# Splitting fp32 operands into words: a ScalarE rounding in place of a VectorE bit mask

## The chip, the cores and the metric

The kernel runs on one core of a Trainium2 chip. A core has five engines that run side by side[...]: TensorE (matmuls; PE in the profile), VectorE (DVE), ScalarE (ACT), GpSimd (POOL) and SyncE, which here only issues DMA. The metric is the time of one execution on the device, in microseconds (us). Before the change it is 3097.36 us, the median of 2 runs (3093.87 to 3100.86). The profile is of one execution with a span of 3092.7 us.

## The reference

A graph layer on 64 graphs of 256 nodes with 768 features, all in fp32. Cut to what matters:

```python
h = maximum(layernorm(x), 0)
ctx = adj @ (h @ Wadj.T + badj) / deg          # adj: 64 x 256 x 256 integers
ctx += adj.T @ (h @ Wrev.T + brev) / rdeg
ctx += h @ Wself.T + bself
out = x + ctx + (terms of the relations)
```

The three 768x768 weights make most of the work. The kernel computes the three weight products as one block product with fewer multiplications than blocks (a scheme of 15 products of sums of blocks). For each graph the left operands are sums of 128-row blocks `a0, a1, a2, b0, b1, b2`, and the right operands are sums of weight blocks, 256 columns wide. The products are made in two sweeps over the 64 graphs: the first makes the aggregates and 8 of the products, and keeps the operands and partial sums in DRAM; the second reloads them and makes the other 7.

## The kernel before

In the second sweep four of the seven products of a graph (9, 7, 15 and 4) are not made as fp32 matmuls but out of shorter words in the type `fp32r`. `split_left` cuts a left operand `value` (128 partitions x 768 fp32) in three words, and it is what the change touches:

```python
def split_left(b, n):
    value = S[b]["L"][PRODUCTS[n][0]]
    words = []                       # three word tiles, from a rotation of three sets of buffers
    for tag in LEFT_WORDS[len(left_words) % 3]:
        ...
    top = pool2.tile([P, F, P], F32, tag="top", name=f"top{n}_{b}")                # SBUF, 2 buffers
    nc.vector.tensor_scalar(top.bitcast(I32), value.bitcast(I32), FIRST, None, op0=ALU.bitwise_and)
    nc.scalar.activation(words[0], top, AF.Copy)
    nc.vector.tensor_tensor(words[1], value, top, op=ALU.subtract)
    nc.vector.scalar_tensor_tensor(words[2], words[1].bitcast(F32), -STEP, top, op0=ALU.mult, op1=ALU.add)
```

`split_right` does the like for the four weight operands, once each, in steps 0 and 1 of the second sweep. The products use the words thus:

```python
def product_first(b, n, ps):                   # 12 short-word matmuls into a PSUM bank
    for k in range(2):
        for f in range(F): nc.tensor.matmul(ps, l[k][:, f, :], r[2 * k][:, f, :], ...)
    nc.scalar.activation(ps, ps, AF.Copy, scale=1.0 + 1.0 / STEP)

def product(b, n, ps, start, row=None):        # 6 more onto the same bank, or 6 in fp32
    ...
def add_out(b, ps, sign, c, n, many=1):        # VectorE: o in SBUF +- a PSUM bank
    nc.vector.tensor_add(o, o, ps)             # or tensor_sub
```

One step of the second sweep (M is the graph being multiplied, A = M+1 the one being prepared; k counts the rows of `ORDER2`, where a product with `None` as its last entry is its `product_first`):

```python
ORDER2 = ((7, "v", None, None), (9, "x", None, ...), (15, "u", None, None), (7, "v", ...), (6, "x", ...),
          (15, "u", ...), (4, "t", None, None), (12, "x", 4, ...), (4, "t", ...), (9, "x", None, None), (1, "x", 5, ...))
for k, (n, *how) in enumerate(ORDER2):
    b = A if (n, how[-1]) == (9, None) else M
    if k == (2 if M < 2 else 0): combine_left(M, "a0+a2+b0+b2")       # GpSimd: one 128x768 addition
    if k == (3 if M == 0 else 0) and A < B: ahead2(A)                 # GpSimd: four more
    multiply(b, n, *how, 2)                                           # matmuls, then their add_out
    if M < 2 and n in WORDS and how[-1] is not None: split_right(n, M)
    if k == 1 and M > 1: split_left(M, 4)
    if 1 < A < B and k in (3, 5, 8): split_left(A, {3: 9, 5: 7, 8: 15}[k])
    ...
```

Products 6, 12 and 1 are plain fp32. Products 9, 6, 12 and 1 share the PSUM bank `x`: each of them adds onto what the last one left, so it must wait until VectorE has read the bank. Instructions go out in program order, and each engine takes its own in that order. The kernel's PSUM tiles are of one bank (2 KB per partition) each: three `q`, three of `ps1` (`pt`, `x`, `y`) and two of `ps2`, whose tile `pa` serves only the first sweep.

Of the kernel before, what the change touches and what calls it, by code (L numbers as in the profile page):

```python
# [9 lines left out]
F32 = mybir.dt.float32  # L10
F32R = mybir.dt.float32r
BF16 = mybir.dt.bfloat16
I32 = mybir.dt.int32
AF = mybir.ActivationFunctionType
ALU = mybir.AluOpType
AX = mybir.AxisListType

P = 128
EPS = 1e-5
NMEAN, RSTD, RDEG, RRDEG = 8, 9, 10, 11  # L20

FIRST = -4096
STEP = 4096.0

# [70 lines left out]
def kernel(  # L97
# [40 lines left out]
    nc = tc.nc  # L138
    B, L, H = x.shape
# [3 lines left out]
    F = H // P  # L143
    HO = H // 2
    NB = H // 3
# [17 lines left out]
    def main_path(main: ExitStack):  # L163
        pool1 = main.enter_context(tc.tile_pool(name="pool1", bufs=1))
        pool2 = main.enter_context(tc.tile_pool(name="pool2", bufs=2))
# [1 line left out]
        dram = main.enter_context(tc.tile_pool(name="dram", bufs=3, space=bass.MemoryType.DRAM))  # L167
        kept = main.enter_context(tc.tile_pool(name="kept", bufs=1, space=bass.MemoryType.DRAM))
        ps3 = main.enter_context(tc.tile_pool(name="ps3", bufs=3, space=bass.MemoryType.PSUM))
        ps2 = main.enter_context(tc.tile_pool(name="ps2", bufs=2, space=bass.MemoryType.PSUM))  # L170
        ps1 = main.enter_context(tc.tile_pool(name="ps1", bufs=1, space=bass.MemoryType.PSUM))

        W = {n: pool1.tile([P, F, NB], F32, name=f"w{n}") for n in PRODUCTS}
        rows = pool1.tile([P, len(ROWS), NB], F32R, name="rows")

        hilo = pool1.tile([P, 2, C, H], F32R, tag="hilo", name="hilo")
# [4 lines left out]
        def load_weights(products):  # L181
            for n in products:
                right = PRODUCTS[n][1]
                k, o = int(right[1]), int(right[2])
                v = (wadj_t, wrev_t, wself_t)[k].rearrange("(f p) o -> p f o", p=P)
                nc.sync.dma_start(W[n], v[:, :, ts(o, NB)])
# [49 lines left out]
        def prepare_rows():  # L236


            eT, brow, pick = (R[n] for n in ("eT", "brow", "pick"))
            wr = R["wr0"], R["wr1"]  # L240
            for k, at in ((0, 1), (1, NBASE + 1)):
                to = pick[:, k, :].rearrange("p (q r) -> p q r", q=4)[:, :, 3 + k]
                nc.scalar.activation(to, eT[:, at : at + 1].to_broadcast([P, 4]), AF.Copy)
            for n in range(2):
                pr = ps2.tile([P, 512], F32, tag="pa", name=f"pr{n}")
                for k in range(2):
                    nc.tensor.matmul(pr[:, :HO], pick[:, k, :], wr[k][:, ts(n, HO)], start=(k == 0), stop=(k == 1))
                nc.vector.tensor_add(brow[:, ts(n, HO)], brow[:, ts(n, HO)], pr[:, :HO])
# [37 lines left out]
        def load_sums(b, sweep):  # L286

            s = S[b]
            s["o"] = pool2.tile([P, C, H], F32, tag="o", name=f"o{sweep}_{b}")
            nc.sync.dma_start(s["o"], x_v[b] if sweep == 1 else s["sums"])  # L290
# [100 lines left out]

        def aggregate(b, f):
            s = S[b]
            pa = ps2.tile([P, 512], F32, tag="pa", name=f"pa_{b}_{f}")
            k = 0
            for c in range(C):
                for part in range(2):
                    nc.tensor.matmul(  # L398
                        pa, hilo[:, part, c, ts(f, P)], s["a"][:, c, :, :].rearrange("p s i -> p (s i)"),
                        start=(k == 0), stop=(k == 2 * C - 1),  # L400
                    )
                    k += 1
            nc.vector.tensor_mul(  # L403
                s["X"][:, f, :, :].rearrange("p s i -> p (s i)"), pa, s["row"][:, 2:4, :].rearrange("p s i -> p (s i)")
            )

        def combine_left(b, name, eng=None):

            L = S[b]["L"]
            x, op, y, home = {**LEFT1, **LEFT2}[name]  # L410
            if home in L:
                L[name] = L[home]
            else:
                L[name] = pool1.tile([P, F, P], F32, tag=home, name=f"{name}_{b}")
            (eng or nc.gpsimd).tensor_tensor(L[name], L[x], L[y], op=op)  # L415

        left_words, right_words = {}, {}

        def split_left(b, n):

            value = S[b]["L"][PRODUCTS[n][0]]
            words = []
            for tag in LEFT_WORDS[len(left_words) % 3]:
                many = 2 if tag == "x" else 1
                pool = pool2 if tag == "a" else pool1
                t = pool.tile([P, many, F, P], F32R, tag=tag, name=f"words{len(words)}_{n}_{b}")
                words += [t[:, k] for k in range(many)]
            top = pool2.tile([P, F, P], F32, tag="top", name=f"top{n}_{b}")
            nc.vector.tensor_scalar(top.bitcast(I32), value.bitcast(I32), FIRST, None, op0=ALU.bitwise_and)  # L429
            nc.scalar.activation(words[0], top, AF.Copy)  # L430
            nc.vector.tensor_tensor(words[1], value, top, op=ALU.subtract)  # L431
            nc.vector.scalar_tensor_tensor(words[2], words[1].bitcast(F32), -STEP, top, op0=ALU.mult, op1=ALU.add)  # L432
            left_words[b, n] = words

        def split_right(n, k):


            work = pool1.tile([P, 2, F, NB], F32, tag="hilo", name=f"work{n}_{k}")
            top, rest = work[:, 0], work[:, 1]
            names = [(f"w{m}", f"w{n}_{i}") for i, m in enumerate((*WORDS[n], n))]  # L440
            tiles = [pool1.tile([P, F, NB], F32R, tag=t, name=m) for t, m in (names[:2] if k == 0 else names[2:])]
            right_words.setdefault(n, []).extend(tiles)
            if k == 0:
                nc.vector.tensor_scalar(top.bitcast(I32), W[n].bitcast(I32), FIRST, None, op0=ALU.bitwise_and)
                nc.scalar.activation(tiles[0], top, AF.Copy)
            nc.vector.tensor_tensor(rest, W[n], top if k == 0 else right_words[n][0].bitcast(F32), op=ALU.subtract)
            if k == 0:
                nc.vector.scalar_tensor_tensor(tiles[1], top, -1.0 / STEP, rest, op0=ALU.mult, op1=ALU.add)
            else:
                nc.scalar.activation(tiles[0], rest, AF.Copy, scale=STEP)  # L450

        def product_first(b, n, ps):
            l, r = left_words[b, n], right_words[n]
            for k in range(2):
                for f in range(F):
                    nc.tensor.matmul(  # L456
                        ps, l[k][:, f, :], r[2 * k][:, f, :], start=(k == 0 and f == 0), stop=(k == 1 and f == F - 1)
                    )
            nc.scalar.activation(ps, ps, AF.Copy, scale=1.0 + 1.0 / STEP)

# [46 lines left out]
        def start():  # L507
# [19 lines left out]
            for f in range(F):  # L527
                aggregate(0, f)
# [87 lines left out]
        def front2(b):  # L616
            s = S[b]
            new_left(b, 2)
            nc.scalar.dma_start(s["X"], s["kept_X"])
            nc.scalar.dma_start(s["Xs"], s["kept_Xs"][:, :, 0, :])  # L620
            line = pool2.tile([P, P], F32, tag="line", name=f"line2_{b}")
            nc.sync.dma_start(line, s["line"])
            s["line2"] = line

        def step2(t):

            M, A = t, t + 1
            s = S[M]
            if A < B:
                load_sums(A, 2)  # L630
            if M > 1 and M + 2 < B:
                front2(M + 2)
            if M == 0:
                front2(1)
            s["tokT"] = pool3.tile([P, P], F32R, tag="tokT", name=f"tokT2_{M}")
            nc.scalar.activation(s["tokT"], s["line2"], AF.Copy)
            for k, (n, *how) in enumerate(ORDER2):
                b = A if (n, how[-1]) == (9, None) else M
                if k == (2 if M < 2 else 0):
                    combine_left(M, "a0+a2+b0+b2")  # L640
                if k == (3 if M == 0 else 0) and A < B:
                    ahead2(A)
                if b < B:
                    multiply(b, n, *how, 2)
                if M < 2 and n in WORDS and how[-1] is not None:
                    split_right(n, M)
                if k == 1 and M > 1:
                    split_left(M, 4)
                if 1 < A < B and k in (3, 5, 8):
                    split_left(A, {3: 9, 5: 7, 8: 15}[k])  # L650
                if how[-1] and n == 4:
                    store_sums(M, 0, 2)
            store_sums(M, 1, 2)
            if M < 2 and M + 2 < B:
                front2(M + 2)

        def ahead2(b):
            for name in ("a0+a2", "a1+a2", "a0+a2+b2", "b1+b2"):
                combine_left(b, name)
# [6 lines left out]
        for t in range(B):  # L666
            step1(t)
            if t == 0:
                load_weights((6, 4, 1))
        ahead2(0)  # L670
        for t in range(B):
            step2(t)
# [123 lines left out]
    with ExitStack() as main:  # L796
        with tc.manual_schedule():
            main_path(main)
# [36 lines left out]
```

## Time and profile before

| | first sweep (0 to 1800 us) | second sweep (2000 to 3000 us) |
|---|---|---|
| TensorE busy | 1725.44 us, 96% | 913.03 us, 91% |
| VectorE busy | 1023.40 us, 57% | 968.32 us, 97% |
| ScalarE busy | 522.13 us, 29% | 254.43 us, 25% |
| GpSimd busy | 1217.00 us, 68% | 605.41 us, 61% |
| DMA rate | 242 GB/s | 210 GB/s |

The busy time of an engine counts an instruction from its start to its end, so time in which a started instruction is held up counts as busy. In the lines of the profile, `L431 DVE TENSOR_TENSOR words<-X,top` is line 431 of the kernel, on VectorE, which writes `words` from `X` and `top`. L429 is the bit mask, L430 the ScalarE copy to the first word, L431 the subtraction, L432 the third word; L415 are the block sums on GpSimd, L456 the matmuls of `product_first`, L468 and L473 those of `product`, L459 the scaling on ScalarE, L481 and L483 the additions into `o`. The fp32 matmul of the program is two matmul instructions in the trace, so six of them show as "x12".

### The profile page before, as it was taken

Reading aid. Unit: us, or ns where it says so; the run is one execution under the profiler, and the core shown is the slowest. Engines: PE = TensorE matmul, PEld = TensorE weight load, DVE = VectorE, ACT = ScalarE, POOL = GpSimd, SP = SyncE. Lnnn points to the kernel's source line nnn. Section 1 sums busy time; section 2 is a strip of 40 time slices with the busy share of each in tenths; the row PEclk is TensorE's granted clock in tenths of the full one; section 3 lists DMA queues with packets and bytes.
Section 4 is the critical chain, followed back from the end, with each engine's and each line's share of the span. In section 5 each row is a group of like instructions: output and inputs, shape, how many; then the busy total and the mean of one; then the engine's idle time right before and its main releaser. Section 6 shows DMA issues by size and latency. Waiting matters only on the chain.

```text
span 3092.7 us, 39494 instructions
## 1 busy us (share of the span) xinstructions
PE 2882.7 (93%) x15002; PEld 2533.7 (82%) x15002; DVE 2220.7 (72%) x3220; ACT 836.7 (27%) x1797; POOL 1965.7 (64%) x905
## 2 busy tenths in 40 slices
PE   5799999999999999999999987999999999999998
PEld 3688888888888888888888876888888888888888
DVE  5655556555555555556565648999999999999997
ACT  3232233223233322323222302222222222222222
POOL 4567767666766777676666654566566565656563
PEclk8899999999999999999999998999999999999999
DMA  8677776777677677766666644655555565555553
GB/s 271 219 249 245 253 246 243 243 240 249 241 254 245 244 247 239 251 237 240 234 233 238 228 158 182 213 207 209 208 208 209 206 213 204 212 208 208 206 209 141
DMA packets 226442, 695.07 MB, mean 225 GB/s; under 512 B 17332, under 2 KB 94900, under 8 KB 209864
## 3 DMA queue, kind: packets, MB, share of 16 engines
q1 hardware_dynamic: 189384, 390.49, 38.1%
q10 hardware_dynamic: 36864, 302.01, 25.8%
q8 instruction: 120, 1.97, 0.3%
q14 instruction: 74, 0.61, 0.1%
HBM read 436.31 MB, written 256.11 MB: 224 GB/s over the span
## 4 chain that ended last, share of the span: by engine, by line
PE 50%; DVE 31%; issue 6%; POOL 5%; DMA 5%; ACT 3%; ACTq 0%; DVEq 0%; SPq 0%; POOLq 0%
PE y L468 17%; DVE words L431 10%; PE w L468 9%; PE pa L398 8%; PE z L468 7%; DVE words L432 6%; DVE top L429 5%; PE x L468 5%; POOL xT L389 5%; DVE o L481 4%; DMA row<-d 3%; PE v L456 1%; DVE o L483 1%; ACT a L307 1%; ACT Xs L390 1%
## 5 line engine op out<-in xcount | busy, mean ns | idle before, releaser
L415 POOL TENSOR_TENSOR X<-X,Xs 128x768 f32<-128x768 f32 x256 | 596.3, 2345 | 511.4 <-DVE words L431 426.9
L389 POOL TENSOR_TENSOR xT<-xT,row 128x1536 f32<-128x1536 f32 (+1 forms) x128 | 445.8, 3483 | 187.2 <-DMA row<-d 182.2
L468 PE MATMUL y<-w,X 128*128 128x256 f32 x2304 | 534.4, 382 | 2.8 <-POOL X L415 2.4
L468 PE MATMUL x<-w,X 128*128 128x256 f32 x1560 | 401.3, 411 | 126.6 <-DVE o L483 86.6
L468 PEld LDWEIGHTS y<-w,X 128*128 128x128 f32 x2304 | 431.2, 191 | 68.6 <-issue 3.5
L398 PE MATMUL pa<-a,hilo 128*128 128x512 f32 x1536 | 455.9, 433 | 26.3 <-DVE X L403 23.3
L468 PEld LDWEIGHTS x<-w,X 128*128 128x128 f32 x1560 | 309.5, 205 | 185.9 <-DVE o L483 98.8
L430 ACT ACTIVATE words<-top 128x768 fp32r<-128x768 f32 x248 | 209.6, 845 | 781.7 <-DVE top L429 781.7
L398 PEld LDWEIGHTS pa<-a,hilo 128*128 128x128 f32 x1536 | 294.4, 192 | 90.6 <-DVE X L403 25.0
L432 DVE SCALAR_TENSOR_TENSOR words<-words,top 128x768 fp32r<-128x768 f32 x248 | 349.4, 1409 | 8.6
L431 DVE TENSOR_TENSOR words<-X,top 128x768 fp32r<-128x768 f32 x186 | 343.7, 1848 | 6.4
L403 DVE TENSOR_TENSOR X<-pa,row 128x512 f32<-128x512 f32 x384 | 264.5, 690 | 115.6 <-PE pa L398 115.3
L390 ACT ACTIVATE Xs<-xT 128x1536 f32<-128x1536 f32 x64 | 95.1, 1485 | 845.5 <-POOL xT L389 845.5
L360 DVE SCALAR_TENSOR_TENSOR hilo<-x,cols,hilo 128x768 fp32r<-128x768 f32 x128 | 261.9, 2047 | 9.8 <-ACT hilo L363 9.7
L320 POOL TENSOR_TENSOR cols<-cols,half 128x2 f32<-128x2 f32 x64 | 44.8, 701 | 251.3 <-DVE cols L319 234.0
L429 DVE TENSOR_SCALAR top<-X 128x768 int32<-128x768 int32 x186 | 187.7, 1009 | 9.0 <-POOL X L415 9.0
L468 PE MATMUL y<-w,b0+b 128*128 128x256 f32 x768 | 178.0, 382 | 2.6 <-POOL b0+b L415 2.6
L468 PE MATMUL x<-w,Xs 128*128 128x256 f32 x768 | 177.0, 380 | 2.7 <-issue 2.7
L468 PE MATMUL z<-w,b2-a 128*128 128x256 f32 x768 | 176.2, 379 | 1.4 <-DVE w L212 1.4
L468 PE MATMUL z<-w,Xs 128*128 128x256 f32 x768 | 176.8, 380 | 0.0
L468 PE MATMUL w<-w,X 128*128 128x256 f32 x768 | 176.3, 379 | 0.0
L468 PE MATMUL w<-w,a1+b 128*128 128x256 f32 x768 | 176.2, 379 | 0.0
(120 smaller groups left out, 4834.1 us busy)
## 6 DMA issues: line engine op xcount, KB each, us to landing
kept_X<-X ACTq DMA_DIRECT2D x64, 1536.0 KB, 5.1
X<-kept_X ACTq DMA_DIRECT2D x64, 1536.0 KB, 7.0
x<-in_x_dram SPq DMA_DIRECT2D x64, 768.0 KB, 6.1
xT<-in_x_t_dram SPq DMA_DIRECT2D x64, 768.0 KB
o<-in_x_dram SPq DMA_DIRECT2D x64, 768.0 KB
kept_Xs<-Xs ACTq DMA_DIRECT2D x64, 768.0 KB, 6.6
sums<-o SPq DMA_DIRECT2D x128, 384.0 KB, 6.8
Xs<-kept_Xs ACTq DMA_DIRECT2D x64, 768.0 KB
```

The source lines that it names most:

```text
L360: nc.vector.scalar_tensor_tensor(lo, hx, rstd, hi.bitcast(F32), op0=ALU.mult, op1=ALU.subtract)
L389: eng.tensor_tensor(v, v, row[:, k : k + 1, :].to_broadcast([P, f1 - f0, L]), op=op)
L390: nc.scalar.activation(s["Xs"], xT, AF.Relu)
L398: nc.tensor.matmul(pa, hilo[:, part, c, ts(f, P)], s["a"][:, c, :, :].rearrange("p s i -> p (s i)"), start=(k == 0), stop=(k == 2 * C - 1),)
L403: nc.vector.tensor_mul(s["X"][:, f, :, :].rearrange("p s i -> p (s i)"), pa, s["row"][:, 2:4, :].rearrange("p s i -> p (s i)"))
L415: (eng or nc.gpsimd).tensor_tensor(L[name], L[x], L[y], op=op)
L429: nc.vector.tensor_scalar(top.bitcast(I32), value.bitcast(I32), FIRST, None, op0=ALU.bitwise_and)
L430: nc.scalar.activation(words[0], top, AF.Copy)
L431: nc.vector.tensor_tensor(words[1], value, top, op=ALU.subtract)
L432: nc.vector.scalar_tensor_tensor(words[2], words[1].bitcast(F32), -STEP, top, op0=ALU.mult, op1=ALU.add)
L468: nc.tensor.matmul(ps, l[:, f, :], r[:, f, :], start=(start and f == 0), stop=(row is None and f == F - 1), skip_group_check=not start,)
L481: nc.vector.tensor_add(o, o, ps)
```

## The change

The first word is no longer made by masking off low bits on VectorE and copying the masked value on ScalarE. ScalarE makes it from the operand itself: it multiplies with 1 - 2^-13 and rounds to `fp32r` as it writes. A second ScalarE instruction copies this word into a PSUM tile, `top`, and VectorE takes its second operand from there in both of its instructions. The aim is to take work off VectorE, and to leave each of its two instructions one operand in SBUF and one in PSUM. The two banks of `pa` are given back at the end of the first sweep, and `top` (3 KB per partition, one buffer in place of two) takes their place. `split_right` gets its first word the same way, but subtracts it from SBUF and makes no copy. The split of product 9 comes one place later in the order. The diff, cut to its core:

```diff
-FIRST = -4096
+LOWER = 1.0 - 2.0**-13
...
-        ps2 = main.enter_context(tc.tile_pool(name="ps2", bufs=2, space=bass.MemoryType.PSUM))
+        sweep = ExitStack()
+        ps_sums = sweep.enter_context(tc.tile_pool(name="ps_sums", bufs=2, space=bass.MemoryType.PSUM))
...                                                                # split_left
-            top = pool2.tile([P, F, P], F32, tag="top", name=f"top{n}_{b}")
-            nc.vector.tensor_scalar(top.bitcast(I32), value.bitcast(I32), FIRST, None, op0=ALU.bitwise_and)
-            nc.scalar.activation(words[0], top, AF.Copy)
+            top = ps_top.tile([P, F, P], F32, tag="top", name=f"top{n}_{b}")
+            nc.scalar.activation(words[0], value, AF.Copy, scale=LOWER)
+            nc.scalar.activation(top, words[0].bitcast(F32), AF.Copy)
             nc.vector.tensor_tensor(words[1], value, top, op=ALU.subtract)
             nc.vector.scalar_tensor_tensor(words[2], words[1].bitcast(F32), -STEP, top, op0=ALU.mult, op1=ALU.add)
...                                                                # split_right
-                nc.vector.tensor_scalar(top.bitcast(I32), W[n].bitcast(I32), FIRST, None, op0=ALU.bitwise_and)
-                nc.scalar.activation(tiles[0], top, AF.Copy)
-            nc.vector.tensor_tensor(rest, W[n], top if k == 0 else right_words[n][0].bitcast(F32), op=ALU.subtract)
+                nc.scalar.activation(tiles[0], W[n], AF.Copy, scale=LOWER)
+            first = right_words[n][0].bitcast(F32)
+            nc.vector.tensor_tensor(rest, W[n], first, op=ALU.subtract)
...                                                                # step2
-                if 1 < A < B and k in (3, 5, 8):
-                    split_left(A, {3: 9, 5: 7, 8: 15}[k])
+                if 1 < A < B and k in (4, 5, 8):
+                    split_left(A, {4: 9, 5: 7, 8: 15}[k])
...                                                                # between the sweeps
+        sweep.close()
+        ps_top = main.enter_context(tc.tile_pool(name="ps_top", bufs=1, space=bass.MemoryType.PSUM))
```

More of the change, by code (lines that the diff above doesn't have):

```diff
@@ L244, in prepare_rows @@
             for n in range(2):
-                pr = ps2.tile([P, 512], F32, tag="pa", name=f"pr{n}")
+                pr = ps_sums.tile([P, 512], F32, tag="pa", name=f"pr{n}")
                 for k in range(2):
@@ L393, in aggregate @@
             s = S[b]
-            pa = ps2.tile([P, 512], F32, tag="pa", name=f"pa_{b}_{f}")
+            pa = ps_sums.tile([P, 512], F32, tag="pa", name=f"pa_{b}_{f}")
             k = 0
@@ L435, in split_right @@
         def split_right(n, k):
-            work = pool1.tile([P, 2, F, NB], F32, tag="hilo", name=f"work{n}_{k}")
-            top, rest = work[:, 0], work[:, 1]
+            rest = pool1.tile([P, F, NB], F32, tag="hilo", name=f"work{n}_{k}")
             names = [(f"w{m}", f"w{n}_{i}") for i, m in enumerate((*WORDS[n], n))]
@@ L443, in split_right @@
             if k == 0:
-                nc.vector.tensor_scalar(top.bitcast(I32), W[n].bitcast(I32), FIRST, None, op0=ALU.bitwise_and)
-                nc.scalar.activation(tiles[0], top, AF.Copy)
-            nc.vector.tensor_tensor(rest, W[n], top if k == 0 else right_words[n][0].bitcast(F32), op=ALU.subtract)
+                nc.scalar.activation(tiles[0], W[n], AF.Copy, scale=LOWER)
+            first = right_words[n][0].bitcast(F32)
+            nc.vector.tensor_tensor(rest, W[n], first, op=ALU.subtract)
             if k == 0:
-                nc.vector.scalar_tensor_tensor(tiles[1], top, -1.0 / STEP, rest, op0=ALU.mult, op1=ALU.add)
+                nc.vector.scalar_tensor_tensor(tiles[1], first, -1.0 / STEP, rest, op0=ALU.mult, op1=ALU.add)
             else:
```

## The prediction

> **What bounds the kernel now.** I read the busy times by stage first, because the change touches only the second sweep (from about 1825 us on) and the shares of the whole page mix both. The columns are TensorE, its weight loads, VectorE, ScalarE and GpSimd, then the granted clock, the DMA share and GB/s.
>
> ```profile
> core 0: us, PE busy (x) PEld busy (x) DVE busy (x) ACT busy (x) POOL busy (x), PEclk, DMA share, GB/s
> 0.00:1800.00 1800.00, 1725.44 (x7885) 1478.93 (x7886) 1023.40 (x1936) 522.13 (x1229) 1217.00 (x582) 0.99 0.70 242
> ...
> 2000.00:3000.00 1000.00, 913.03 (x5738) 835.58 (x5738) 968.32 (x1042) 254.43 (x470) 605.41 (x260) 0.98 0.59 210
> ```
>
> The first sweep is TensorE's. In the second VectorE is busy 97% of the time, and TensorE is down to 91%. Which of them ends last is told by the chain of waits of that stretch, and by its list of waits:
>
> ```profile
> by line: DVE words L431 28.1%; DVE words L432 14.9%; DVE top L429 14.3%; issue 13.5%; DVE o L481 11.5%; PE x L468 11.2%; PE v L456 3.6%; DVE o L483 2.6%; PE x L473 0.3%; DVEq L481 0.1%; DVEq L429 0.0%
> ```
>
> ```profile
> ACT words L430 <- DVE top L429: 658.3, 209, 6.1
> POOL X L415 <- DVE words L431: 374.9, 51, 8.6
> PEld x L468 <- DVE o L483: 86.4, 52, 2.1
> PE x L468 <- DVE o L483: 75.7, 52, 1.9
> ```
>
> VectorE holds 71% of the chain, and 57% are the three lines of the split. ScalarE and GpSimd wait for the same lines. TensorE waits once in each of the 52 steps of the stretch (a step is 1000/52 = 19.23 us), and for VectorE. Next I asked what one split costs, with the shapes kept apart (busy, mean ns of one):
>
> ```profile
> L432 DVE SCALAR_TENSOR_TENSOR words<-words,top 128x768 fp32r<-128x768 f32 x208 | 294.5, 1416 | 7.2
> L431 DVE TENSOR_TENSOR words<-X,top 128x768 fp32r<-128x768 f32 x156 | 289.5, 1856 | 5.4
> L429 DVE TENSOR_SCALAR top<-X 128x768 int32<-128x768 int32 x156 | 155.1, 994 | 0.0
> L431 DVE TENSOR_TENSOR words<-Xs,top 128x768 fp32r<-128x768 f32 x53 | 50.8, 959 | 1.8
> ```
>
> The same subtraction takes 959 ns in one group and 1856 in the other. The timeline shows why: with GpSimd at rest it takes 0.96 us, and beside a run of GpSimd additions 2.46.
>
> ```profile
> 2214.88 0.96 DVE L431 TENSOR_TENSOR words<-X,top 128x768 fp32r<-128x768 f32 x1
> ...
> 2215.99 7.15 POOL L415 TENSOR_TENSOR X<-X,Xs 128x768 f32<-128x768 f32 x3 [8.56 <-DVE words L431]
> ...
> 2218.98 2.46 DVE L431 TENSOR_TENSOR words<-X,top 128x768 fp32r<-128x768 f32 x1
> ```
>
> Lastly, what TensorE could do if nothing held it. The last steps of the run have no GpSimd work left, so they show it; before them is one that waited:
>
> ```profile
> 3030.51 4.54 PE L468 MATMUL x<-w,X 128*128 128x256 f32 x12 [1.78 <-DVE o L483]
> ...
> 3050.77 4.54 PE L468 MATMUL x<-w,X 128*128 128x256 f32 x12 [1.76 <-DVE o L483]
> 3054.96 0.47 PE L473 MATMUL x<-rows,tokT 128*128 128x256 f32 x1
> 3055.27 1.60 PE L456 MATMUL v<-w,words 128*128 128x256 f32 x12
> ...
> 3069.13 2.75 PE L468 MATMUL x<-w,X 128*128 128x256 f32 x12
> 3071.53 0.47 PE L473 MATMUL x<-rows,tokT 128*128 128x256 f32 x1
> 3071.84 1.58 PE L456 MATMUL v<-w,words 128*128 128x256 f32 x12
> ```
>
> From `v` to `v` that is 3071.84 - 3055.27 = 16.57 us for a whole step, with no idle. In a step that waits, the wait costs 1.76 us and the twelve matmuls after it run in 4.54 us, not 2.75.
>
> [...]lines L481 and L483, with one operand in PSUM, support it: 0.41 us in nearly every place of the timeline, GpSimd busy or not.[...]
>
> **The change part by part, for one step.**
>
> *Removed from VectorE.* Four masks: (155.1 + 29.3)/52 = 3.55 us (29.3 is the group on Xs, 553 ns each). The other instructions stay, but should lose their contention. The four subtractions now take (289.5 + 50.8)/52 = 6.54 us, the four third words 294.5/52 = 5.66. With a PSUM operand I take 0.96 us each: the 256 and 512 wide additions from PSUM take 0.41 and 0.68, so 0.27 per 256 more, which carries to 0.95 at 768. Eight of them are 7.7. With the additions into `o`, 199.0/52 = 3.83 us and unchanged, VectorE goes from 15.75 + 3.83 = 19.6 us (18.6 busy, as successive ones overlap slightly) to 11.5 of a step.
>
> *Added to ScalarE.* The rounding takes the place of the old copy: 0.85 us. The copy into PSUM is new: 0.85 by the same row. Four splits add 3.4 us. With four scalings of 0.37 and one 0.31, ScalarE goes from 254.43/52 = 4.9 to 8.3 us. It has room, but it lies in the path of each split.
>
> *GpSimd.* Its additions average 2.33 us in this stretch (605.41/260). In the first sweep, where VectorE leaves it alone, the like take 1.82 (612.70 to 614.53, one of many). Five are 9.1 in place of 11.6 us.
>
> *TensorE.* Nothing changes: 16.57 us. It is now the longest of the four.
>
> *Does a wait take its place?* I laid out one step by hand, with time 0 at the end of product 6 (k=4): VectorE adds bank `x` to `o` (0.4) and makes split 9 (1.9); ScalarE may then copy the next `top` (0.85), VectorE makes split 7 (1.9) and reads bank `x` after product 12 (0.4). That is 5.5 us, and about 6 with the hops. TensorE needs the bank for product 1 after products 15, 4, 12, 4 and 9: 0.7 + 1.4 + 2.7 + 0.7 + 1.4 = 6.9 us. So it holds, with about 1 us to spare. The scaling of `t`, behind ScalarE's copies for split 7, has about the same.
>
> *Sum.* From `v` at 1938.73 to `v` at 3055.27 there are 58 steps of 19.25 us. At 16.57 they give back 58 x 2.68 = 155 us. I put back 0.2 us per step (12 us) for waits not foreseen. The four steps before take 31, 30, 29 and 19 us, because TensorE stands some 10 us in each of the first three: once behind `split_right`, whose masks of 2.40 and 1.96 us go, and twice because VectorE takes up split 9, which awaits GpSimd and a reload, before the read of bank `x` behind it. With that split one place later the read comes first. I estimate 4 + 5 + 5 us, less than those waits, as the reloads stay. The first sweep is as it was. 3097 - 155 + 12 - 14 = 2940; I say **2940 us**, 5% less.
>
> **Rivals.** (1) *Latency replaces throughput:* `top` has one buffer, so the ScalarE copy, subtraction and third word of one split must end before the next copy, and ScalarE's own order puts the scalings behind it. For it: only 1 us is spare, by hand. Against: about half of ScalarE's step stays free. If each step lost 1 us: 2990. (2) *The DMA:* the reloads and stores of a step move 210 GB/s now, and at 16.6 us they would need 210 x 19.23/16.6 = 243. `o` can be loaded only after the store before it has landed. Against: the first sweep sustains 242. If it cost 0.5 us a step: 2970. (3) *A PSUM operand [...]reads slower:* then only the masks go, 3.55 us less the contention that shifts to others; VectorE still falls to about 15 to 16 us, below TensorE: 2960 to 2990. (4) *No gain, or a loss,* would need ScalarE's two copies to take twice their time, 3 us each split; nothing in the trace speaks for it.
>
> **Range and chances.** The floor is 16.57 us a step with half of the 30 us of starting waits gone: 2915. Rivals 1 to 3 alone end at 2960 to 2990. I give 2908 to 2992. Within 2% would need over 3035, where less than 62 of the 155 us come. Faster by over 2%: 0.94; within: 0.045; slower: 0.015.
>
> **What would show it.** Steps of 16.6 to 16.9 us between 2000 and 3000; TensorE over 96% there and VectorE near 70%; the successors of L431 and L432 all near 0.96 us, none at 2.46; GpSimd additions at 1.82; ScalarE near 50%; no twelve matmuls of 4.54 us. Wrong would be: TensorE waiting each step for ScalarE's scaling or for VectorE behind a ScalarE copy (rival 1), VectorE waiting for the load of `o` (rival 2), or two sorts of subtraction as before (rival 3).

## The result, and the profile after

The changed kernel takes 2934.6 us (median of 2 runs, 2932.43 to 2936.77): 0.9475 of the time before, with a 95% interval of 0.942 to 0.9529. Run again beside the experiments it took 0.9475 (0.9444 to 0.9506). The prediction was 2940 us, with a range of 2908 to 2992.

The busy times by stage of the changed kernel, in the columns used before (TensorE, its weight loads, VectorE, ScalarE, GpSimd, granted clock, DMA share, GB/s):

```profile
0.00:1800.00 1800.00, 1716.61 (x7851) 1469.63 (x7852) 1024.59 (x1932) 522.07 (x1229) 1214.27 (x579) 0.99 0.69 241
...
2000.00:2800.00 800.00, 800.00 (x5318) 754.91 (x5317) 531.67 (x772) 385.92 (x631) 433.75 (x240) 1.00 0.68 243
```

TensorE is busy for all of the 800 us in the second sweep; VectorE has fallen from 97% to 66%, ScalarE has risen from 25% to 48%. The chain of waits of that stretch has no other engine left in it:

```profile
by line: PE x L469 51.2%; PE u L457 8.8%; PE v L457 8.6%; PE x L457 8.6%; PE t L457 8.5%; PE v L469 4.4%; PE u L469 4.3%; PE t L469 4.2%; PE x L474 1.4%
```

The groups of the split and of GpSimd's additions in the same stretch (busy, mean ns of one, then idle time before them). L431 is now the rounding, L432 the copy into PSUM, L433 the subtraction and L434 the third word:

```profile
L417 POOL TENSOR_TENSOR X<-X,Xs 128x768 f32<-128x768 f32 x192 | 348.8, 1835 | 357.4 <-DVE words L433 350.7 <-DMA Xs<-kept_Xs 4.9 <-issue 1.8
...
L434 DVE SCALAR_TENSOR_TENSOR words<-words,top 128x768 fp32r<-128x768 f32 x193 | 184.1, 954 | 6.7
L432 ACT ACTIVATE top<-words 128x768 f32<-128x768 f32 x194 | 158.3, 816 | 198.4 <-DVE words L434 195.5 <-DVE o L484 1.4
L433 DVE TENSOR_TENSOR words<-X,top 128x768 fp32r<-128x768 f32 x144 | 137.1, 952 | 20.4 <-POOL X L417 19.4 <-ACT top L432 0.9
...
L431 ACT ACTIVATE words<-X 128x768 fp32r<-128x768 f32 x145 | 120.7, 832 | 0.0
```

Both VectorE instructions take 0.95 us whatever GpSimd does (of the 386 in this stretch 129 run beside its additions from end to end and 146 beside none, and each one lies between 947 and 957 ns); before they averaged 1.86 (on X) and 1.42. GpSimd's additions fell from 2.36 us, in the line below from 2000 to 3000 us of the kernel before, to 1.84:

```profile
L415 POOL TENSOR_TENSOR X<-X,Xs 128x768 f32<-128x768 f32 x208 | 486.5, 2355 | 391.9 <-DVE words L431 374.9 <-DMA Xs<-kept_Xs 15.4 <-issue 1.4
```

A full step went from 19.25 to 16.56 us. In the changed kernel the 58 steps lie between these two starts of product 7:

```profile
1932.70 1.58 PE L457 MATMUL v<-w,words 128*128 128x256 f32 x12
...
2893.17 1.60 PE L457 MATMUL v<-w,words 128*128 128x256 f32 x12
```

So the 162 us between the two spans are 58 x 2.69 = 156 from the full steps, and 13 from the four steps before them; against these stand 7 us of the first sweep, which the change does not touch: its end, taken as the start of the first product 7, lay anywhere between 1825 and 1858 us in the traces of this study.

### The profile page after: what moved, and what is told of

It reads as the page before. It is cut to its first block, busy times and chain, and to the rows that moved or that the text cites. A ratio compares the mean times of both kernels' runs of the same rounds, so it can differ in the third digit from the quotient of the medians.

```text
span 2930.6 us, 39745 instructions
## 1 busy us (share of the span) xinstructions
PE 2821.0 (96%) x15002; PEld 2504.8 (85%) x15002; DVE 1748.8 (60%) x2968; ACT 1027.8 (35%) x2045; POOL 1809.4 (62%) x905
## 4 chain that ended last, share of the span: by engine, by line
PE 78%; POOL 6%; DMA 6%; DVE 5%; ACT 3%; issue 1%; ACTq 0%; SPq 0%; POOLq 0%; DVEq 0%
PE x L469 18%; PE y L469 18%; PE w L469 9%; PE pa L400 8%; PE z L469 7%; POOL xT L391 6%; DMA row<-d 4%; PE x L457 3%; PE u L457 3%; PE v L457 3%; PE t L457 3%; PE t L469 2%; PE u L469 1%; PE v L469 1%; ACT a L309 1%; DVE cols L330 1%
## 5 line engine op out<-in xcount | busy, mean ns | idle before, releaser
L417 POOL TENSOR_TENSOR X<-X,Xs 128x768 f32<-128x768 f32 x256 | 469.6, 1853 | 500.0 <-DVE words L433 435.6
L469 PE MATMUL x<-w,X 128*128 128x256 f32 x1560 | 362.1, 382 | 14.7 <-POOL X L417 10.0
L469 PEld LDWEIGHTS x<-w,X 128*128 128x128 f32 x1560 | 289.6, 192 | 50.6 <-POOL X L417 10.4
L432 ACT ACTIVATE top<-words 128x768 f32<-128x768 f32 x248 | 202.3, 816 | 248.9 <-DVE words L434 245.4
L434 DVE SCALAR_TENSOR_TENSOR words<-words,top 128x768 fp32r<-128x768 f32 x248 | 236.5, 954 | 8.6
L433 DVE TENSOR_TENSOR words<-X,top 128x768 fp32r<-128x768 f32 x186 | 177.1, 952 | 43.3 <-POOL X L417 34.9
L469 PEld LDWEIGHTS z<-w,b2-a 128*128 128x128 f32 x768 | 145.4, 189 | 24.2 <-DVE w L214 1.8
```

Of the source, the lines that this page charges most:

```text
L432: nc.scalar.activation(top, words[0].bitcast(F32), AF.Copy)
L469: nc.tensor.matmul(ps, l[:, f, :], r[:, f, :], start=(start and f == 0), stop=(row is None and f == F - 1), skip_group_check=not start,)
```

## The experiments

Times below are ratios to the kernel before, with 95% intervals, and the step is the mean from one product 7 to the next between 2000 and 2800 us.

| kernel | ratio | step, us |
|---|---|---|
| before | 1 | 19.25 |
| the change, run again | 0.9475 (0.9444 to 0.9506) | 16.56 |
| copy in SBUF | 0.9645 (0.9606 to 0.9684) | 17.6 |
| no copy | 0.9663 (0.9635 to 0.9692) | 17.6 |
| mask kept, copy of it in PSUM | 1.0508 (1.0466 to 1.055) | 21.7 |
| the same, PSUM copy first | 1.0276 (1.0231 to 1.0321) | 20.5 |
| the same, masks sent ahead | 0.9808 (0.9761 to 0.9855) | 18.2 |
| the change in the old order | 0.9503 (0.9462 to 0.9545) | 16.6 |
| the new order alone | 1.0245 (1.0198 to 1.0291) | 20.5 |
| two copies into PSUM | 0.9602 (0.9577 to 0.9628) | 17.3 |
| three copies into PSUM | 1.0324 (1.0297 to 1.0351) | 20.9 |
| second copy beside the chain | 0.9465 (0.9434 to 0.9497) | 16.56 |
| earlier reload | 0.9428 (0.9403 to 0.9453) | 16.56 |

The theory: VectorE was the bound by what it had to do and by the longer time of its instructions beside GpSimd's additions (2.46 us against 0.96), and the change takes away both. The rivals: the masks taken away did it alone (theory A below); the second operand in PSUM, with which the instructions take 0.95 us beside GpSimd too, did it alone (theory B); the order did it; or something else that the sum of work does not show.

First, the changed kernel once more.

> The changed kernel itself, once more, so that the runs beside it have it on the same chip: 0.947 of the time before, 2930 to 2950 us.

### Undoing the PSUM half

Two kernels keep the rounding on ScalarE but give VectorE two SBUF operands. For the first, theory A has 2935 to 2965 us and theory B over 3010.

```diff
 # copy in SBUF
-            top = ps_top.tile([P, F, P], F32, tag="top", name=f"top{n}_{b}")
+            top = pool2.tile([P, F, P], F32, tag="top", name=f"top{n}_{b}")
 # no copy
-            nc.scalar.activation(top, words[0].bitcast(F32), AF.Copy)
+            top = words[0].bitcast(F32)
```

> The changed kernel with one thing undone: the copy of the first word lies in SBUF (two buffers), so VectorE has as few instructions as in the changed kernel but two SBUF operands in each. If the masks taken away are what matters (theory A), VectorE has at most 6.54 + 5.66 + 3.83 = 16.0 us of a step, TensorE 16.55, and the time is 2935 to 2965 us. [...]subtractions of 2.46 us come back at the wrong moments and the step stays near 18 us: over 3010 us. I expect 2955, with subtractions and GpSimd additions of two sorts again.

> The changed kernel without the copy: VectorE takes the first word itself from SBUF. ScalarE has 3.3 us less of a step, VectorE two SBUF operands. If contention decides, the same as the run with the copy in SBUF, within 10 us; if the length of the chain through ScalarE decides, faster than that by 10 us or more.

They took 0.9645 and 0.9663: about two thirds of the gain, and the same within their intervals. The first, at 2999.64 us, landed between the two theories' ranges and well above the 2955 expected, so neither half is the whole. From the timeline of the kernel with the copy in SBUF:

```profile
2207.39 7.53 POOL L417 TENSOR_TENSOR X<-X,Xs 128x768 f32<-128x768 f32 x3 [5.02 <-DVE words L433]
...
2208.75 1.98 DVE L433 TENSOR_TENSOR words<-X,top 128x768 fp32r<-128x768 f32 x1
...
2210.77 2.48 DVE L434 SCALAR_TENSOR_TENSOR words<-words,top 128x768 fp32r<-128x768 f32 x1
...
2213.17 0.41 DVE L484 TENSOR_TENSOR o<-o,x 128x256 f32<-128x256 f32 x1
...
2213.63 2.86 PE L469 MATMUL x<-w,X 128*128 128x256 f32 x12 [0.74 <-DVE o L484]
```

Beside the run of GpSimd additions the two instructions take 1.98 and 2.48 us again, the read of bank `x` behind them comes late, and TensorE waits 0.74 us for it. GpSimd pays as well: its additions average 2.55 us here. VectorE's sum was not the limit: 703.64 us in 800, 15.5 us a step, would fit under TensorE's 16.56; what came too late was that one read. That the kernel with no copy, which takes 3.3 us a step off ScalarE, is no better shows that the copy costs nothing in these two kernels; what they share, and the change does not, is the second operand in SBUF.

### The PSUM half alone

The mask stays on VectorE, and ScalarE makes from it the first word and a copy in PSUM (order of the splits as in the changed kernel).

```diff
             nc.vector.tensor_scalar(top.bitcast(I32), value.bitcast(I32), FIRST, None, op0=ALU.bitwise_and)
             nc.scalar.activation(words[0], top, AF.Copy)
+            masked = top
+            top = ps_top.tile([P, F, P], F32, tag="ptop", name=f"ptop{n}_{b}")
+            nc.scalar.activation(top, masked, AF.Copy)
```

> The kernel before with the other half alone: the mask stays on VectorE in SBUF, ScalarE makes the first word from it as before and a second copy of it in PSUM, from which VectorE subtracts (order of the splits as in the changed kernel). Theory B: VectorE has 4 x (0.9 + 0.95 + 0.95) + 3.83 = 15 us of a step, the step is TensorE's, and the time 2935 to 2965. Theory A: the masks, still in contention with GpSimd (2.1 us at times), hold VectorE near 18 us: over 3010. I expect 2955, from 1.1 us spare before the bank x is needed and a chain longer by the mask.

It was 5% slower than the kernel before, and both theories are wrong about it. It is over the 3010 us of theory A, but not by its reason: VectorE has only 511.73 us of work in 800, 14 us a step. Its timeline in one step, from product 6 to the second part of product 4:

```profile
2204.59 2.75 PE L472 MATMUL x<-w,Xs 128*128 128x256 f32 x12
...
2213.24 0.87 DVE L430 TENSOR_SCALAR top<-X 128x768 int32<-128x768 int32 x1
2214.20 0.84 ACT L431 ACTIVATE words<-top 128x768 fp32r<-128x768 f32 x1 [3.46 <-DVE top L430]
2214.95 0.80 ACT L434 ACTIVATE ptop<-top 128x768 f32<-128x768 f32 x1
2215.69 0.34 ACT L463 ACTIVATE t<-t 128x256 f32<-128x256 f32 x1
2215.78 0.95 DVE L435 TENSOR_TENSOR words<-X,ptop 128x768 fp32r<-128x768 f32 x1 [1.67 <-ACT ptop L434]
...
2216.08 1.65 PE L472 MATMUL t<-w,words 128*128 128x256 f32 x6 [3.90 <-ACT t L463]
```

Each split is a round trip: VectorE masks, then stands 1.67 us while ScalarE makes two copies, then goes on. Nothing fills that time: VectorE waits for the copy 148 times in the 800 us, 247.7 us in all. ScalarE scales `t` only after both copies of split 7 (2214.20, 2214.95 and 2215.69 above). That the engines keep to the order of the program is seen in the kernel before and in the changed one, where VectorE, ScalarE and GpSimd each show one and the same sequence in every step compared (50 and 46 steps from 2000 us on). So TensorE waits for the scaled `t`, 3.90 us here (3.54 in the median step). Two more kernels shorten the trip: one copies into PSUM first, and one sends each mask with its copies some places ahead of the subtraction. If a second operand in PSUM, without the wait for ScalarE, is all that is needed, the latter should have the whole gain of the change.

```diff
 # PSUM copy first
-            nc.scalar.activation(words[0], top, AF.Copy)
             masked = top
             top = ps_top.tile(...)
             nc.scalar.activation(top, masked, AF.Copy)
+            nc.scalar.activation(words[0], masked, AF.Copy)
 # masks sent ahead (begin_left: mask and both copies; end_left: subtraction and third word)
+                if k == 0 and M > 1: begin_left(M, 4)
+                if k == 1 and M > 1: end_left(M, 4)
+                if 1 < A < B:
+                    if k == (1 if M > 2 else 4): begin_left(A, 9)
+                    if k in (4, 5, 8): end_left(A, {4: 9, 5: 7, 8: 15}[k])
+                    if k in (4, 6): begin_left(A, {4: 7, 6: 15}[k])
```

> The mask kept and its copy in PSUM, as in the run that took 1.051 of the time before, but with ScalarE's copy into PSUM ahead of the one to the first word. There VectorE stands 1.67 us in each split between its mask and its subtraction, while ScalarE makes both copies. With this order it stands 0.8: 4 x 0.84 = 3.4 us less of a step of 21.6, so some 205 us less: 3040 to 3070. If something else made that run slow (the masks in contention), it stays over 3200.

> The mask kept and its copy in PSUM, but each mask and its two ScalarE copies go out some places ahead of the subtraction and third word of the same split (4 at k=0 and 1, 9 at 1 and 4, 7 at 4 and 5, 15 at 6 and 8), so VectorE need not stand while ScalarE copies. VectorE has 4 x (0.9 + 1.9) + 3.8 = 15.0 us of a step, below TensorE's 16.55. [...]the gain of the change comes with the masks still there: 2935 to 2960. If the masks themselves must go: over 3000.

Both expectations were too hopeful. The list of waits of the kernel with the PSUM copy first, over its 39 steps from 2000 to 2800 us (us in total, times, longest):

```profile
DVE words L435 <- ACT ptop L433: 138.4, 157, 0.9
...
PE t L472 <- ACT t L463: 87.2, 39, 2.3
DVE o L485 <- PE x L472: 83.1, 78, 1.7
```

VectorE does stand only 0.88 us in each split, as expected, but the step fell by 1.2 us and not by 3.4. The rest went into other waits: VectorE now waits 2.1 us a step for product 6 or 9, and TensorE still 2.2 us for the scaled `t`. With the masks ahead the kernel comes to 0.9808, faster than before and well short of the change. Its 3045 us are over the 3000 that were to mean that the masks themselves must go; but VectorE is busy for only 606.97 us of the 800, and the timeline shows ScalarE as the place where time is lost:

```profile
2210.37 0.55 DVE L432 TENSOR_SCALAR top<-X 128x768 int32<-128x768 int32 x1
2210.84 0.68 DVE L493 TENSOR_TENSOR o<-o,v 128x512 f32<-128x512 f32 x1
2211.02 0.84 ACT L433 ACTIVATE words<-top 128x768 fp32r<-128x768 f32 x1 [2.54 <-DVE top L432]
2211.77 0.80 ACT L435 ACTIVATE ptop<-top 128x768 f32<-128x768 f32 x1
...
2212.50 0.34 ACT L471 ACTIVATE u<-u 128x256 f32<-128x256 f32 x1
...
2212.89 0.97 PE L480 MATMUL u<-w,words 128*128 128x256 f32 x6 [0.83 <-ACT u L471]
```

ScalarE waits 2.54 us for the mask, which is itself behind split 4 on VectorE, and the scaling of `u` stands in line behind it. So with the mask in place the PSUM operand alone was never seen to give the gain of the change; the value of the PSUM operand is read from the kernels with the copy in SBUF, and is about a third. That third goes down to TensorE's 16.56 us a step, so it says what the operand is worth in this kernel and not what it would be worth where TensorE has more to spare.

### The order

```diff
 # the change in the old order
-                if 1 < A < B and k in (4, 5, 8):
-                    split_left(A, {4: 9, 5: 7, 8: 15}[k])
+                if 1 < A < B and k in (3, 5, 8):
+                    split_left(A, {3: 9, 5: 7, 8: 15}[k])
 # the new order alone: the reverse, in the kernel before
```

> The changed kernel with the split of product 9 back in its old place (k=3). By my working the full steps do not depend on it (VectorE has the time between products 7 and 6), so they stay at 16.55 us, and only the steps 1 and 2, where VectorE takes up the split before it may read bank x, lose about 10 us together: 2940 to 2950. If the order is needed in each step, 0.5 us or more in 61 steps: over 2965.

> The kernel before with the new place of the split alone. VectorE's work is the same, so full steps stay at 19.2 us; steps 1 and 2 gain up to 10 us: 3085 to 3097. If the order matters much in itself, because the read of bank x comes sooner and TensorE's wait of 1.7 us a step goes: under 3030.

In the changed kernel the order makes no difference that these runs resolve (0.9503, and 0.9475 for the change), near what was expected. In the kernel before, the new order costs 2.5%, 3182.72 us where 3085 to 3097 was expected, though VectorE's instructions are the same. Its timeline:

```profile
2200.26 2.75 PE L468 MATMUL x<-w,Xs 128*128 128x256 f32 x12
...
2203.05 0.42 DVE L481 TENSOR_TENSOR o<-o,x 128x256 f32<-128x256 f32 x1 [0.99 <-PE x L468]
...
2206.44 1.57 DVE L429 TENSOR_SCALAR top<-X 128x768 int32<-128x768 int32 x1
...
2208.05 0.84 ACT L430 ACTIVATE words<-top 128x768 fp32r<-128x768 f32 x1 [3.22 <-DVE top L429]
...
2208.80 0.37 ACT L459 ACTIVATE t<-t 128x256 f32<-128x256 f32 x1
...
2209.22 0.99 PE L468 MATMUL t<-w,words 128*128 128x256 f32 x6 [1.36 <-ACT t L459]
```

VectorE, the bound of that kernel, first stands 0.99 us for product 6, which it did not do with split 9 ahead of that read; then split 9 and the mask of split 7 come behind it, and so does everything on ScalarE. The same path can be measured in each trace: the time from the end of product 6 to the end of the scaling of `t`. TensorE itself needs about 4.85 us from there until it wants `t` (products 15, 4 and 12; 2204.70 to 2209.54 in the changed kernel). The values are medians over the steps from 2000 to 2800 us.

| kernel | product 6 to scaled `t`, us | less 4.85 | TensorE's wait for `t` |
|---|---|---|---|
| the change | 3.5 | none | none |
| before | 4.8 | none | none |
| two copies into PSUM | 5.2 | 0.35 | 0.41 |
| masks sent ahead | 5.8 | 0.95 | none, but 0.83 for `u` just before |
| the new order alone | 6.2 | 1.3 | 1.36 |
| PSUM copy first | 7.0 | 2.2 | 2.24 |
| three copies into PSUM | 7.7 | 2.9 | 2.94 |
| mask kept, copy in PSUM | 8.3 | 3.5 | 3.54 |

The path ends at what TensorE waits for, so the columns must agree; what the table shows is how little room there was. The kernel before has next to none, and the new order lengthens its path by 1.4 us. (The new order alone also waits 1.76 us a step for the read of bank `x`, behind a subtraction of 2.45 us and a third word of 2.47 beside GpSimd's additions; that wait the kernel before has too, 1.5 us a step.) This path is what the sums of busy time do not show, and what makes the change more than a shorter list of work: when ScalarE starts a split by itself, it runs ahead while VectorE is busy elsewhere, and only its last copy lies on the path. In the changed kernel's step at 2204 us the rounding for split 7 starts at 2204.08, before VectorE has begun split 9 (2205.07), and ScalarE then waits 2.19 us for VectorE's last read of `top` before the copy at 2207.10.

### How much was to spare

```diff
             nc.scalar.activation(top, words[0].bitcast(F32), AF.Copy)
+            nc.scalar.activation(top, words[0].bitcast(F32), AF.Copy)      # two copies (three: once more)
 # second copy beside the chain, in its place:
+            beside = pool2.tile([P, F, P], F32, tag="beside", name=f"beside{n}_{b}")
+            nc.scalar.activation(beside, words[0].bitcast(F32), AF.Copy)
```

> The changed kernel with ScalarE's copy into PSUM made twice, so each split takes 0.82 us longer on its way and ScalarE has 3.3 us more of a step. In the trace of the changed kernel TensorE takes bank x for product 1 about 1.2 us after VectorE has read it, and the scaled t 1.2 us after ScalarE is done with it. So nothing is lost: 2930 to 2942. If the one buffer or ScalarE's order is already at its limit (rival 1), up to 0.8 us a step: 2960 to 2985.

> The same with three copies, 1.64 us more in each split. That is 0.4 us over what is spare, so 0.4 to 0.6 us in each of 61 steps: 2955 to 2975. If the spare time is larger than the trace suggests, no change; if ScalarE becomes the bound (8.0 + 6.6 = 14.6 us, with its waits), more than 2990.

> The changed kernel with a second ScalarE copy in each split, as in the run with two copies, but to an SBUF tile that nobody reads, after the copy into PSUM: ScalarE has the same work more (3.3 us of a step), and the chain copy, subtraction, third word, next copy is as short as in the changed kernel. If the run with two copies lost its time by that chain through the one buffer, this one loses less than 0.2 us a step: 2930 to 2945. If by ScalarE's load or order, it loses the same 0.7 us a step: 2970 to 2985.

The first two expectations failed: 0.82 us more in each split cost 0.7 us a step and not nothing, and 1.64 us cost 4.4 us and not 0.5. I had counted one copy on the path where the one buffer puts several: the copy for split 9 must wait for VectorE's last read of split 4, that for split 7 for the last of split 9, so each lengthening comes in more than once. The path from product 6 to the scaled `t` grew by 1.7 us with 0.82 us more in a split, and by 4.2 with 1.64. In the kernel with two copies:

```profile
2209.57 0.81 ACT L432 ACTIVATE top<-words 128x768 f32<-128x768 f32 x1 [1.36 <-DVE words L435]
2210.41 0.82 ACT L433 ACTIVATE top<-words 128x768 f32<-128x768 f32 x1
...
2211.16 0.34 ACT L461 ACTIVATE t<-t 128x256 f32<-128x256 f32 x1
...
2211.56 0.98 PE L470 MATMUL t<-w,words 128*128 128x256 f32 x6 [0.40 <-ACT t L461]
```

The third kernel gives ScalarE the same extra work, but off that path, and it shows which of the two it was. TensorE stays busy for the whole stretch, with ScalarE at 66%:

```profile
2000.00:2800.00 800.00, 800.00 (x5314) 754.79 (x5313) 533.48 (x775) 527.62 (x823) 438.92 (x244) 1.00 0.68 242
```

It took 0.9465, as expected for that case. So ScalarE's load was not the limit; the chain of copies ahead of VectorE was. That the single buffer is what ties it is read from the waits (`top` waits for `words` of the split before, 1.36 us above); two buffers of `top` were not tried.

### The waits at the start

Three waits are left where the second sweep begins (changed kernel):

```profile
1849.47 4.43 PE L469 MATMUL x<-w,X 128*128 128x256 f32 x12 [4.64 <-DVE o L482]
...
1879.72 4.67 PE L469 MATMUL x<-w,X 128*128 128x256 f32 x12 [10.05 <-POOL X L417]
...
1908.61 1.65 PE L469 MATMUL t<-w,words 128*128 128x256 f32 x6 [4.98 <-ACT t L460]
```

The last kernel gives graph 2 the third set of operand buffers, which is free as soon as `split_right` keeps its scratch in the room that the old `top` left, so that its reload can start with the sweep.

```diff
-            third = sweep == 2 and b % 3 == 0 and b > 0
+            third = sweep == 2 and b % 3 == 2
-            rest = pool1.tile([P, F, NB], F32, tag="hilo", name=f"work{n}_{k}")
+            rest = pool1.tile([P, F, NB], F32, tag="rest_right", name=f"work{n}_{k}")
-            if M > 1 and M + 2 < B:
-                front2(M + 2)
             if M == 0:
                 front2(1)
+            if M + 2 < B:
+                front2(M + 2)
 ...
-            if M < 2 and M + 2 < B:
-                front2(M + 2)
```

> The changed kernel with the third set of operand buffers given to graph 2 and not to graph 3, and split_right's scratch in the room that the old top left in SBUF, so that the reload of graph 2 goes out at the start of the second sweep and that of graph 3 one step sooner. The waits of 10 us in step 1 and of 5 us in step 2 are waits for those reloads by my reading: 2915 to 2922. If they are waits for VectorE's splits of the weights in truth, 2930 to 2936.

Its waits in the start of the sweep:

```profile
1849.28 4.51 PE L469 MATMUL x<-w,X 128*128 128x256 f32 x12 [4.65 <-DVE o L482]
...
1870.86 2.83 PE L469 MATMUL x<-w,X 128*128 128x256 f32 x12 [0.98 <-DVE o L482]
...
1883.75 4.56 PE L469 MATMUL x<-w,X 128*128 128x256 f32 x12 [5.94 <-DVE o L484]
```

The wait of 10 us was for the reload: it is down to 0.98, and the one of 4.98 us, a step later, is gone. The first was not: there VectorE makes the splits of the weights, with instructions of up to 3.24 us, ahead of the read of bank `x`. A new wait of 5.94 us of the same sort has come up in step 1, so of 15 us of waiting 8 are won. The four steps at the start take 10.3 us less, 85.5 (1836.69 to 1922.20) against 95.8 (1836.89 to 1932.70; 96.0 in the repeat of the change). It took 2925.6 us, 0.9428, where 2915 to 2922 was expected; that is the best of the study, but its interval just touches that of the change. The traces show 10 us, 0.3%; more than that is not shown.

## Why the prediction was right

**The step.** TensorE's 16.57 us, read from a step at the end of the run where GpSimd had no more work, is 16.56 in the changed kernel, and TensorE is the bound. This carried the prediction: 155 us were expected from the full steps, and 156 came.

**The work of each engine.** VectorE 11.5 us a step expected, 531.67 us in 48.3 steps = 11.0 measured; ScalarE 8.3 and 8.0 (the 0.85 us for each of its instructions in a split came from L430, 845 ns in the kernel before; the rounding takes 832 and the copy 816); GpSimd 9.1 and 9.0. The PSUM operand takes 0.95 us, as worked out from the 256 and 512 wide reads. The DMA rate needed is 243 GB/s, and 243 was moved (rival 2 fell). What spoke ahead of the result for a PSUM operand that keeps its time beside GpSimd was the additions into `o` of the kernel before: from 2000 to 3000 us those 256 wide take 0.41 us beside GpSimd's additions and away from them, those 512 wide 0.68 in both places. For the 768 wide instructions of the split it is now shown by the two groups above: 337 VectorE instructions, at 952 and 954 ns in the mean, with GpSimd busy for 433.75 us of the 800. By what mechanism two SBUF operands lengthen both engines' instructions is not shown.

**The new wait.** The layout by hand gave 5.5 to 6 us from product 6 to the read of bank `x` after product 12, with 6.9 until TensorE wants it; the trace has 5.6 (2204.70 to 2210.29) and 6.8. So rival 1 did not come. But the spare time was less than the layout made it look: taken as 1 us for a longer copy, it did not hold 0.82, because the layout started at product 6 and let only one copy lie on the path. For the change this made no difference; for the two kernels with more copies it was the step that failed.

**The start.** 4 + 5 + 5 = 14 us were expected and 13 came, but not in those places: steps 0 to 3 gained 6.2, 0.5, 4.3 and 2.2 us. The step that put 5 us on step 1, the earlier read of bank `x`, was wrong: the wait there is for the reload, as the last experiment shows, and the new order earns nothing that could be measured. Step 3, from which nothing extra was expected, gave 2.2. So that the two sums agree is luck.

**The number.** That only 5 us lie between 2940 and 2934.6 is partly luck as well: the 12 us put back for unforeseen waits were not needed, and the 7 us by which the first sweep was longer in the changed kernel's trace hid more than half of that. The floor of 2915 us counts the four starting steps at 16.57 us too; the terms of the sum alone, 3097 - 155 - 15, give 2927.

**Rival 3.** If the PSUM operand had brought VectorE no relief from GpSimd's additions, or had been read more slowly, 2960 to 2990 was said; the kernels with SBUF operands, 0.9645 and 0.9663 of 3097 us, are at 2987 and 2993, its upper end. So the masks, or what goes with them, are two thirds of the gain, and the PSUM operand one third. The sum of VectorE's work behind that rival was right (15 to 16 us a step, 15.5 measured with the copy in SBUF), but it did not bring the step down to TensorE's 16.56.

## What to carry to other kernels

Read what the next engine would take for a stage from a place in the trace where nothing holds it; that figure, and not the work removed, is where a gain ends. Before adding up busy times, draw the path that closes over a step through the engines, each in the order of its instructions: work moved to another engine was hidden here only where that engine could start it without waiting for the first, and a trip there and back lay on the path though both engines were idle for over a third of the time (the kernel with the mask kept, where VectorE is busy for 511.73 us of 800 and ScalarE for 282.70). A second operand in PSUM kept VectorE and GpSimd out of each other's way here (0.95 us against up to 2.48 on VectorE, additions of 1.84 against 2.55 on GpSimd), but with a single buffer between two engines a longer copy came in two and three times on one path.

## What was not expected of the hardware

After waits of nearly the same length TensorE goes on at two speeds. In the kernel before, after waits of 1.76 to 1.78 us for VectorE, the next twelve matmuls took 4.54 us in some steps and 2.86 in others, against 2.75 with no wait. The granted clock (the number after the five engines) tells the two apart. The first line is a stretch that begins 0.66 us after the start of twelve matmuls that took 4.54 us, the second covers twelve that took 2.86:

```profile
2204.72:2208.13 3.41, 3.41 (x10) 2.67 (x9) 3.38 (x2) 1.12 (x2) 2.71 (x2) 0.50 0.33 120
2224.34:2227.20 2.86, 2.86 (x14) 2.55 (x15) 2.83 (x4) 1.11 (x2) 2.86 (x2) 1.00 0.35 138
```

Between 2000 and 2800 us of that kernel, all 11 groups of 4.54 us fall into stretches of 3.4 us at a clock of 0.5, and none of the 22 of 2.86 us after waits of over 1 us does. Such stretches came in the kernels in which TensorE waited 1.7 us or more at one place in most steps (before, the new order alone, and those at 1.0508, 1.0276 and 1.0324), and not between 2000 and 2800 us in the others, whose waits there stayed under 1.4 us. In the three slowest the clock averaged 0.92 to 0.93, so such a kernel loses more than the waits themselves: in the kernel with the mask kept, 22 of 36 waits for `t` were followed by six matmuls in about 1.65 us, where the changed kernel takes 0.87. Why one wait is followed by such a stretch and the next one is not stays open.
